# Sums moved into the slots' bank, the steps of a pass reordered, beginning and end rewritten: a graph-attention layer on one core

## The chip, the cores and the metric

The kernel runs on one core of a Trainium2 chip. The metric is the device time of one execution in microseconds (us). The core has a matrix engine (TensorE, "PE" in the profile, with its weight loads as "PEld"), three engines for element-wise work (VectorE "DVE", ScalarE "ACT", GpSimd "POOL") and SyncE ("SP"), which here only starts transfers. GpSimd starts the gathers: one instruction fetches 128 rows of 128 floats by 128 indices. TensorE writes its results into PSUM, which the kernel divides into banks of 128 x 512 floats; VectorE and ScalarE read them from there. Every engine works through its own instructions in order and waits for others by semaphores.

## The reference

12,500 nodes with 128 features, 200,000 edges sorted by target node, so about 16 edges per node. What is computed, cut to what matters:

```python
h = jnp.maximum(_layernorm(x, axis=-1), 0.0)
Qv = h @ W_Q.T;  Ku = h @ W_K.T
score = jnp.einsum('md,md->m', Qv[dst], Ku[src]) * (1.0 / np.sqrt(d))
score = score * jnp.exp(-edge_dt)
...                                   # per target node: keep the 16 best scores
w = jnp.where(keep, jnp.exp(score_m - seg_max[dst_s]), 0.0)
alpha = w / denom[dst_s]
msgs = h[src_s] @ W_msg.T
agg = segment_sum(alpha[:, None] * msgs, dst_s)
return x + jax.nn.relu(h @ W_self.T + agg)
```

## The kernel before

**Tiling.** The edges are cut into 1,563 chunks of 128, and 14 chunks (GC) make a group; there are G = 112 groups, the last one (L = 111) with 9 chunks. A group is also given the first chunk of the next one (NJ = 15), and it owns up to 128 target nodes. For every edge the row h[src] is gathered into the tile hs of its group (line 176, one instruction per chunk); eight such tiles exist.

**Preparation** (to line 421). `src` is loaded, cast (335), turned by TensorE and written as columns of indices (338). x is loaded in six blocks; VectorE takes row statistics (`row_stats`, line 200 and after), ScalarE the square root (212) and the normalised rows (`normed`, 220), and SyncE stores them as h_tab. The first four groups (RAW) don't wait for h_tab: their rows are gathered from x itself (`gather_at_once`) and normalised later in the tile (`raw_stats`, `raw_normed`). Then `dst` is turned into distances and places: `rel` (381), a running count (the scan, 386), and the table pd, with 16 places and 16 distances for every edge and group (397 and 400), which is made of transposes in TensorE's three "q" banks. The table is [edge, group, 2, 16], so that one write of many groups is strided.

**Passes** (lines 709 to 785). A software pipeline, written out by hand: the order of the calls in a pass is the order on every engine. Pass i works on several groups at once:

- group i + 2: node rows turned (`h_turned`, `h_turned_out`, line 517), then q = h A (`q_made`, `q_out`).
- group i + 1: the "eight steps of nodes and distances". Four `far_of` (TensorE to bank "a", line 534; ScalarE squares it out, 536), `edges_turned` (547, 550) and three `away` (557, 559). All go through the single bank "a", so each waits until ScalarE has read the step before. `to_edges` (541) and `places` (563) end them.
- group i: `q_to_edges` (574) carries q to the edges, `scores` (583) multiplies with the gathered rows and sums; `scores_in_slots` (591) spreads the scores over 40 slots.
- group i - 1: `slots_by_node` (599) sums the slots of each node into bank "e", columns 0 to 151; `slots_out` (604) and `node_by_slots` (607) turn them into columns 256 to 296 of the same bank.
- group i - 2: `best` (613 to 625) finds the 16 best, `sum_of_exps` (630), `kept_to_edges` (642), `one_over_sum`, `on_edges` (648 to 655) and `exps` bring the result back to the edges.
- group i - 3: `weights` (663, 664), then `sums` (674), the weighted sum of h[src] on TensorE, in bank "a" in two halves, and `sums_out` (679).
- groups i - 4 and i - 5: `sums_turned`, `products` (689, 690) in bank "s"; `output` (694) and `store` (700 on SyncE; 703 on GpSimd for the last four groups).

Between them `more(k)` lets gathers go: VectorE copies two columns of indices (191), and GpSimd starts two gathers. In pass i these are gathers of groups i + 4 and i + 5, for pass 3 the first of group 8, which takes over the tile of group 0. In the first four passes `raw_stats` and `raw_normed` for group i + 1 stand in the pass, and the entries of `later` (checks on the input, lines 440 to 451) are spread over passes 1 to 9. The loop runs to i = G + 5, so the last six passes only finish what is in the pipeline.

Lines 789 and after are a general path that is taken only if a check fails; it isn't taken here.

## Time and profile before

| | |
|---|---|
| time, median of 3 runs | 2059.91 us (2058.63 to 2059.99) |
| the profiled execution | 2061.69 us, of which its span is 2059.8 |
| granted TensorE clock, mean | 0.906 of full speed |
| busy: PE / PEld / DVE / ACT / POOL | 1641.5 / 1314.4 / 1274.5 / 1044.7 / 1513.8 us |
| first gather, last gather, last store started | 15.76, 2014.06, 2046.57 us |
| granted clock, 100 to 200 us | 0.73 |

A line of a group's table gives the line of the program, engine, operation, tiles and shapes, the count, the busy time and the mean duration in ns, and the idle time just before these instructions with what ended it. A line of a timeline gives the start and duration in us, then the same, and in brackets the idle time before and what ended it. L12 is line 12 of the kernel before.

### The profile page before, as it was taken

To read this page: it belongs to the slowest core of one execution; us is meant where nothing else is said; L and a number is where in the kernel's file an instruction comes from. 1 tells how busy PE (TensorE), PEld (TensorE's weight loads), DVE (VectorE), ACT (ScalarE), POOL (GpSimd) and SP (SyncE) were. 2 spreads that over 40 slices of the span, in tenths; PEclk is the share of its full clock that TensorE was granted. 3 is DMA by queue.
4 is the path that set the end of the run, shared out by engine and by line. 5 is a ranking of instruction groups with operands and counts; after the bars stand their busy time and mean duration, and the time that the engine had idled before them with its cause. 6 is when DMAs were issued, how large, how long until landed. Compare 5 with 4: busy or idle time off the path is not lost. (4 is left out here: it accounts for less than half of the span.)

```text
span 2059.8 us, 42100 instructions
## 1 busy us (share of the span) xinstructions
PE 1641.5 (80%) x13800; PEld 1314.4 (64%) x13801; DVE 1274.5 (62%) x6998; ACT 1044.7 (51%) x2198; POOL 1513.8 (73%) x1580
## 2 busy tenths in 40 slices
PE   0367899999887888888888888878888778888885
PEld 0246677777676766667666666766666666667664
DVE  7547767676666555565656666566556655666653
ACT  6756555565444554444544544454444544445440
POOL 6775777777777777777777777777777777777771
PEclk9958999999989898898989999899989998898987
DMA  9521222222222222222222222222222222222220
GB/s 237 158 57 46 74 69 64 69 65 68 65 63 63 64 66 64 64 65 65 65 65 65 65 64 63 64 65 65 65 65 65 65 65 65 65 65 63 64 55 16
DMA packets 101472, 143.46 MB, mean 70 GB/s; under 512 B 31063, under 2 KB 74327, under 8 KB 100480
## 3 DMA queue, kind: packets, MB, share of 16 engines
q0 software_dynamic: 50144, 102.74, 19.1%
q1 hardware_dynamic: 51102, 37.99, 6.7%
q8 instruction: 108, 1.77, 0.4%
q14 instruction: 118, 0.97, 0.2%
HBM read 126.79 MB, written 14.40 MB: 69 GB/s over the span
## 5 line engine op out<-in xcount | busy, mean ns | idle before, releaser
L176 POOL DMA_INDIRECT hs<-h_tab,ix x1507 | 1445.7, 959 | 475.4 <-issue 298.3
L583 DVE SCALAR_TENSOR_TENSOR prod<-hs,dec_all,q 128x128 f32<-128x128 f32 x1674 | 499.8, 344 | 193.0 <-DMA hs<-h_tab,ix 159.4
L574 PEld LDWEIGHTS q<-q,to_e 128*128 128x128 f32 x3348 | 477.4, 215 | 73.7 <-issue 59.6
L574 PE MATMUL q<-q,to_e 128*128 128x128 f32 x3348 | 520.4, 303 | 0.0
L536 ACT ACTIVATE far<-a,minus 128x512 bf16<-128x512 f32 (+1 forms) x447 | 295.2, 660 | 390.5 <-PE a L534 381.2
L674 PE MATMUL a<-hs,alz 128*128 128x128 f32 x3348 | 444.1, 288 | 11.5 <-ACT aw L559 0.4
L674 PEld LDWEIGHTS a<-hs,alz 128*128 128x128 f32 x3348 | 413.8, 201 | 22.6 <-ACT aw L559 19.2
L613 DVE TENSOR_SCALAR ell<-slots,e 128x40 f32<-128x40 f32 x112 | 29.7, 265 | 467.9 <-PE e L599 449.9
L599 PEld LDWEIGHTS e<-opo,sl 128*41 128x41 f32 x3348 | 177.3, 133 | 100.5 <-issue 89.4
L534 PE MATMUL a<-rel,ident 112*128 112x512 bf16 (+1 forms) x447 | 191.4, 428 | 44.1 <-ACT far L536 27.0
L559 ACT ACTIVATE aw<-a 128x400 bf16<-128x400 f32 x336 | 168.6, 502 | 106.8 <-PE a L557 106.8
L599 PE MATMUL e<-opo,sl 128*41 128x40 f32 x3348 | 217.8, 223 | 0.0
L541 ACT ACTIVATE to_e<-far 128x1920 f32<-128x1920 bf16 x112 | 200.5, 1790 | 0.0
L557 PE MATMUL a<-minus_at,pdT 32*128 32x400 bf16 x336 | 118.0, 351 | 95.2 <-ACT aw L559 78.8
L682 PE MATMUL s<-ident,agn 128*128 128x128 f32 x112 | 40.1, 358 | 172.1 <-DVE o L694 168.1
L679 ACT ACTIVATE agn<-a,rden 128x128 f32<-128x128 f32 x112 | 41.2, 368 | 198.3 <-PE a L674 198.3
L583 DVE DVE_READ_ACCUMULATOR prod<-hs,dec_all,q 128x1 f32 x1674 | 138.5, 83 | 0.0
L563 ACT ACTIVATE opo<-aw 128x1200 f32<-128x1200 bf16 x112 | 136.1, 1215 | 0.0
L682 PEld LDWEIGHTS s<-ident,agn 128*128 128x128 f32 x112 | 16.5, 147 | 185.4 <-DVE o L694 178.4
L191 DVE COPY ix<-idx_all 128x2 int32<-128x2 int32 x754 | 129.7, 186 | 0.0
L642 PEld LDWEIGHTS <-to_e 128*128 128x128 bf16 x1674 | 51.6, 99 | 100.3 <-DVE prod L583 86.9
L550 ACT CAST pdT<-a 32x128 bf16<-32x128 f32 x112 | 28.5, 254 | 157.5 <-PE a L547 157.5
(172 smaller groups left out, 1734.8 us busy)
## 6 DMA issues: line engine op xcount, KB each, us to landing
hs<-h_tab,ix POOLq DMA_INDIRECT x1507
h_r<-h_tab SPq DMA_DIRECT2D x112, 64.0 KB
x_t<-in_x_dram SPq DMA_DIRECT2D x108, 64.0 KB
out_dram<-o SPq DMA_DIRECT2D x108, 64.0 KB
xg<-in_x_dram SPq DMA_DIRECT2D x2, 1400.0 KB
h_tab<-xg SPq DMA_DIRECT2D x2, 1400.0 KB
xg<-in_x_dram SPq DMA_DIRECT2D x1, 1120.0 KB
h_tab<-xg SPq DMA_DIRECT2D x1, 1120.0 KB
```

The source lines that it names most:

```text
L176: nc.gpsimd.indirect_dma_start(out=T[g]["hs"][:, j, :], out_offset=None, in_=table[0:N, :], in_offset=bass.IndirectOffsetOnAxis(ap=index(j ...
L191: nc.vector.tensor_copy(ix[:, j0:j1], idx_all[:, GC * g + j0:GC * g + j1])
L534: nc.tensor.matmul(pr[:, 0:n1 - n0], lhsT=upper(ident[0:RR, g:g + 1]).to_broadcast([RR, P]), rhs=rel[:, n0:n1], start=True, stop=True)
L536: nc.scalar.activation(T[g]["far"][:, n0:n1], pr[:, 0:n1 - n0], AF.Square, bias=minus)
L541: nc.scalar.activation(T[g]["to_e"][:, 0:n], T[g]["far"][:, 0:n], AF.Relu, bias=1.0, scale=-1.0)
L557: nc.tensor.matmul(pr[:, 0:400], lhsT=T[g]["pdT"], rhs=minus_at.rearrange("k w j s -> k (w j s)")[:, n0:n1], start=True, stop=True)
L559: nc.scalar.activation(T[g]["aw"][:, n0:n1], pr[:, 0:400], AF.Square)
L563: nc.scalar.activation(T[g]["opo"].rearrange("e w j s -> e (w j s)"), T[g]["aw"], AF.Relu, bias=1.0, scale=-1.0)
L574: nc.tensor.matmul(pq[:, (j - j0) * P:(j - j0 + 1) * P], lhsT=T[g]["to_e"][:, j * P:(j + 1) * P], rhs=T[g]["q"], start=True, stop=True)
L583: nc.vector.scalar_tensor_tensor(prod, rows_of(g, j), dec_all[:, c:c + 1], T[g]["pq", b][:, (j % 4) * P:(j % 4 + 1) * P], op0=OP.mult, op1 ...
L599: nc.tensor.matmul(et[0:KM + 1, STEP * j:STEP * j + WN], lhsT=sl1[g % 2][:, j, :], rhs=T[g]["ow"][:, j, :], start=False, stop=(j == n - 1))
L674: nc.tensor.matmul(T[g]["pa"][:, 0:P], lhsT=alz[g % 2][:, WW * j + PRE:WW * j + PRE + P], rhs=rows_of(g, j), start=(j == 0), stop=(j == n ...
```

## The change

- **Beginning.** The GpSimd instructions that make `slots`, `nvec` and `jj` come ahead of those for `dst_r`. Memsets of w0, alz[0] and sl1 move behind the normalising of x, and most of the memset of pd is dropped. The cast of src is cut into 512 columns and the rest. The statistics of the first block of x follow the first gathers. `raw_stats` and `raw_normed` of groups 0 and 1 move out of the passes into the preparation; those of groups 2 and 3 become `raw_stats` and one tile (`raw_begun`) at the end of pass 0 and 13 tiles (`raw_finished`) at the end of passes 1 and 2.
- **Table turned.** pd is [edge, 32, group]: the writes of 397 and 400 are contiguous, and the columns that `edges_turned` loads are strided.
- **Passes.** `sums` goes to columns 384 to 511 of bank "e", so bank "a" serves only the eight steps, which spread over the pass; the three blocks of `slots_by_node` stand together; `node_by_slots` and `edges_turned` move to the middle of the pass, `sums_out` ahead of `products`; q has two buffers, not three.
- **End.** The loop stops after pass G - 2, and what remains is one written list.

```diff
--- before.py
+++ after.py
...
-    pd = const.tile([P, G, 2, 16], BF16, name="pd")
-    dlw = pd[:, :, 1, 0:NJ]
+    pd = const.tile([P, 32, G], BF16, name="pd")
+    dlw = pd[:, 16:16 + NJ, :].rearrange("e j g -> e g j")
...
-    def normed(rows, n, rs, sm):
-
-        nc.vector.reciprocal(rs, rs)
-        nc.vector.scalar_tensor_tensor(sm, sm, -0.5, rs, op0=OP.mult, op1=OP.mult)
-        for t in range(n):
+    def normed(rows, n0, n1, rs, sm):
+
+        if n0 == 0:
+            nc.vector.reciprocal(rs, rs)
+            nc.vector.scalar_tensor_tensor(sm, sm, -0.5, rs, op0=OP.mult, op1=OP.mult)
+        for t in range(n0, n1):
             nc.scalar.activation(rows[:, t, :], rows[:, t, :], AF.Relu, bias=sm[:, t:t + 1],
                                  scale=rs[:, t:t + 1])
+
+
+    def raw_stats(g):
+        T[g]["raw"] = row_stats(rows_pool, T[g]["hs"], own[g], f"r{g % 2}")
+
+    def raw_normed(g):
+        normed(T[g]["hs"], 0, own[g], *T[g]["raw"])
+
+
+    def raw_begun(g):
+        normed(T[g]["hs"], 0, 1, *T[g]["raw"])
+
+    def raw_finished(g):
+        normed(T[g]["hs"], 1, own[g], *T[g]["raw"])
...
         make_identity(nc, ident)
+        nc.gpsimd.iota(slots, pattern=[[1, KM]], base=0, channel_multiplier=0,
+                       allow_small_or_imprecise_dtypes=True)
+        nc.gpsimd.iota(nvec, pattern=[[0, 1]], base=0, channel_multiplier=1,
+                       allow_small_or_imprecise_dtypes=True)
+
+        jj, eq = (alz[0][0:32, NJ * KM * k:NJ * KM * (k + 1)].rearrange("p (j k) -> p j k", k=KM) for k in range(2))
+        nc.gpsimd.iota(jj, pattern=[[1, NJ], [0, KM]], base=0, channel_multiplier=0,
+                       allow_small_or_imprecise_dtypes=True)
         nc.gpsimd.iota(dst_r, pattern=[[1, RL + P]], base=1 << 21, channel_multiplier=0)
...
-        nc.gpsimd.iota(slots, pattern=[[1, KM]], base=0, channel_multiplier=0,
-                       allow_small_or_imprecise_dtypes=True)
-        nc.gpsimd.iota(nvec, pattern=[[0, 1]], base=0, channel_multiplier=1,
-                       allow_small_or_imprecise_dtypes=True)
...
-        nc.vector.memset(pd, 1.0)
+        for k in (15, 31):
+            nc.vector.memset(pd[:, k, :], 1.0)
+        nc.vector.memset(pd[:, GC:NJ, G - 1:G], 0.0)
         nc.vector.memset(dec_all[:, RR * CPR:CW], 0.0)
         nc.vector.tensor_scalar(minus, nvec, -1.0, None, op0=OP.mult)
-        for j in range(NJ):
-            nc.vector.memset(w0[:, j:j + 1], float(lead(j)))
...
-        nc.vector.memset(alz[0], 0.0)
-        for k in range(2):
-            nc.vector.memset(sl1[k][:, :, KM:], 1.0)
-
 
         src_f = src_r.bitcast(F32)[:, 0:RW]
-        nc.vector.tensor_copy(src_f, src_r[:, 0:RW])
-        stat = {0: row_stats(prep, xs[0][2], sizes[0], "x0")}
+        nc.vector.tensor_copy(src_f[:, 0:4 * P], src_r[:, 0:4 * P])
+        nc.vector.tensor_copy(src_f[:, 4 * P:], src_r[:, 4 * P:RW])
         by_chunk = lambda t: t[:, 0:RR * CPR].rearrange("e (p j) -> e j p", j=CPR)
         to_columns(src_f, 0, lambda at, p: nc.vector.tensor_copy(at(by_chunk(idx_all)), p))
-        for g in range(min(RAW, G)):
+        for g in range(RAW):
             gather_at_once(g, x)
+        stat = {0: row_stats(prep, xs[0][2], sizes[0], "x0")}
...
-            normed(xg, n, *stat[i])
+            normed(xg, 0, n, *stat[i])
...
+        for j in range(NJ):
+            nc.vector.memset(w0[:, j:j + 1], float(lead(j)))
+        nc.vector.memset(alz[0], 0.0)
+        for k in range(2):
+            nc.vector.memset(sl1[k][:, :, KM:], 1.0)
+        for g in range(2):
+            raw_stats(g)
...
+        raw_normed(0)
...
+        raw_normed(1)
...
-            nc.vector.tensor_tensor(dlw.rearrange("e g j -> e j g")[:, j0:j1, :],
+            nc.vector.tensor_tensor(pd[:, 16 + j0:16 + j1, :],
                                     pt[:, 0:(j1 - j0) * RR].rearrange("e (j g) -> e j g", g=RR),
                                     bc(w0[:, j0:j1], RR), op=OP.subtract)
-        to_columns(h1, HALO, lambda at, p: nc.scalar.copy(at(pd[:, :, 0, :].rearrange("e g j -> e j g")), p))
-        nc.scalar.copy(pd[:, 0:G - 1, 0, GC:NJ], pd[:, 1:G, 0, 0:1])
+        to_columns(h1, HALO, lambda at, p: nc.scalar.copy(at(pd), p))
+        nc.scalar.copy(pd[:, GC:NJ, 0:G - 1], pd[:, 0:1, 1:G])
...
-            T[g]["q"] = win.tile([P, D], F32, name="q", bufs=3)
+            T[g]["q"] = win.tile([P, D], F32, name="q", bufs=2)
...
-            nc.tensor.matmul(pr[0:32, 0:P], lhsT=pd[:, g, :, :].rearrange("e w j -> e (w j)"), rhs=upper(ident),
+            nc.tensor.matmul(pr[0:32, 0:P], lhsT=pd[:, :, g], rhs=upper(ident),
...
-            if part == 0:
-                T[g]["pa"] = bank("a", 1)
             half = n // 2
             for j in range(half) if part == 0 else range(half, n):
-                nc.tensor.matmul(T[g]["pa"][:, 0:P], lhsT=alz[g % 2][:, WW * j + PRE:WW * j + PRE + P],
+                nc.tensor.matmul(et[:, 384:384 + P], lhsT=alz[g % 2][:, WW * j + PRE:WW * j + PRE + P],
                                  rhs=rows_of(g, j), start=(j == 0), stop=(j == n - 1))
 
         def sums_out(g):
             T[g]["agn"] = win.tile([P, D], F32, name="agn")
-            nc.scalar.activation(T[g]["agn"], T[g]["pa"][:, 0:P], AF.Copy, scale=T[g]["rden"])
+            nc.scalar.activation(T[g]["agn"], et[:, 384:384 + P], AF.Copy, scale=T[g]["rden"])
...
-        for i in range(-3, G + 6):
+        for i in range(-3, G - 1):
...
-            if i + 1 < RAW:
-                at(i + 1, raw_stats)
-
...
             at(i, q_to_edges, 0)
-            at(i + 1, edges_turned)
             at(i - 5, output)
             at(i - 5, store)
             at(i - 3, weights)
@@ -741,48 +750,130 @@
...
             at(i, q_to_edges, 1)
             at(i + 1, far_of, 1)
-            at(i - 1, slots_by_node, 0)
+            for b in range(3):
+                at(i - 1, slots_by_node, b)
             at(i + 1, far_of, 2)
-            at(i - 1, slots_by_node, 1)
-            at(i + 1, far_of, 3)
-            at(i - 1, slots_by_node, 2)
-            at(i + 1, away, 0)
-            if i + 1 < RAW:
-                at(i + 1, raw_normed)
             more(1)
             at(i - 2, best)
             more(2)
             at(i - 2, sum_of_exps)
             at(i - 1, slots_out)
             at(i, q_to_edges, 2)
-            at(i + 1, away, 1)
+            at(i + 1, far_of, 3)
             at(i + 2, h_turned)
-            at(i + 1, away, 2)
             at(i, scores, 0)
             more(3)
             at(i + 1, to_edges)
             at(i + 2, h_turned_out)
             at(i - 2, kept_to_edges)
+            at(i - 1, node_by_slots)
+            at(i + 1, edges_turned)
             at(i - 3, sums, 0)
             at(i, scores, 1)
             more(4)
+            at(i + 1, away, 0)
             at(i, q_to_edges, 3)
             at(i - 2, one_over_sum)
+            at(i + 1, away, 1)
             at(i - 3, sums, 1)
             at(i, scores, 2)
             at(i - 2, on_edges)
             more(5)
+            at(i + 1, away, 2)
+            at(i - 3, sums_out)
+            at(i - 4, products)
+            at(i - 2, exps)
             at(i + 1, places)
-            at(i - 4, products)
-            at(i - 3, sums_out)
-            at(i - 2, exps)
             at(i, scores, 3)
             at(i, scores_in_slots)
+            if i == 0:
+                raw_stats(2)
+                raw_stats(3)
+                raw_begun(2)
+                raw_begun(3)
+            if i in (1, 2):
+                raw_finished(i + 1)
             more(6)
-            at(i - 1, node_by_slots)
             at(i + 2, q_made)
             if i > 0 and later:
                 later.pop(0)()
+
+
+        L = G - 1
+        blocks = -(-chunks[L] // 4)
+
+        def turned(g):
+            sums_turned(g)
+            sums_turned_out(g)
+
+        def all_sums(g):
+            sums(g, 0)
+            sums(g, 1)
+            sums_out(g)
+
+        def to_rows(g):
+            products(g)
+            output(g)
+            store(g)
+
+        def all_slots(g):
+            for b in range(3):
+                slots_by_node(g, b)
+
+        def to_nodes(g):
+            all_slots(g)
+            slots_out(g)
+            node_by_slots(g)
+
+        def kept_on_edges(g):
+            one_over_sum(g)
+            on_edges(g)
+            exps(g)
+
+        q_to_edges(L, 0)
+        output(L - 5)
+        store(L - 5)
+        weights(L - 3)
+        turned(L - 4)
+        all_slots(L - 1)
+        slots_out(L - 1)
+        best(L - 2)
+        sum_of_exps(L - 2)
+        q_to_edges(L, 1)
+        node_by_slots(L - 1)
+        to_rows(L - 4)
+        all_sums(L - 3)
+        kept_to_edges(L - 2)
+        best(L - 1)
+        sum_of_exps(L - 1)
+        scores(L, 0)
+        kept_on_edges(L - 2)
+        turned(L - 3)
+        kept_to_edges(L - 1)
+        scores(L, 1)
+        weights(L - 2)
+        all_sums(L - 2)
+        to_rows(L - 3)
+        for b in range(2, blocks):
+            q_to_edges(L, b)
+            scores(L, b)
+        scores_in_slots(L)
+        to_nodes(L)
+        kept_on_edges(L - 1)
+        turned(L - 2)
+        best(L)
+        sum_of_exps(L)
+        weights(L - 1)
+        kept_to_edges(L)
+        all_sums(L - 1)
+        to_rows(L - 2)
+        kept_on_edges(L)
+        turned(L - 1)
+        weights(L)
+        all_sums(L)
+        to_rows(L - 1)
+        turned(L)
+        to_rows(L)
     assert not later
     order.close()
 
```

More of the change, by code (lines that the diff above doesn't have):

```diff
@@ L112, in gnn_layer @@
     G = -(-CH // GC)
-    assert G > TAIL
+    assert G > TAIL + 2
     EG = GC * P
@@ L298, in gnn_layer @@
         load_rows(ew_r, ew)
-        nc.gpsimd.iota(slots, pattern=[[1, KM]], base=0, channel_multiplier=0,
-                       allow_small_or_imprecise_dtypes=True)
-        nc.gpsimd.iota(nvec, pattern=[[0, 1]], base=0, channel_multiplier=1,
-                       allow_small_or_imprecise_dtypes=True)
-        jj, eq = (alz[0][0:32, NJ * KM * k:NJ * KM * (k + 1)].rearrange("p (j k) -> p j k", k=KM) for k in range(2))
-        nc.gpsimd.iota(jj, pattern=[[1, NJ], [0, KM]], base=0, channel_multiplier=0,
-                       allow_small_or_imprecise_dtypes=True)
         nc.gpsimd.memset(alz[1], 0.0)
@@ L447, in gnn_layer @@
                                                op1=OP.mult, accum_out=badc[:, 2:3]),
-        lambda: nc.vector.tensor_reduce(badc[:, 0:1], pd[:, :, 0, 0:NJ], axis=AX.XY, op=OP.max),
+        lambda: nc.vector.tensor_reduce(badc[:, 0:1], pd[:, 0:NJ, :], axis=AX.XY, op=OP.max),
         lambda: nc.vector.tensor_scalar(badc[:, 0:1], badc[:, 0:1], float(KM), None, op0=OP.is_ge),
@@ L502, in load_nodes @@
                 nc.sync.dma_start(T[g]["x_t"], x_end[ds(start_of(g, 1, XT), P), :])
-        def raw_stats(g):
-            T[g]["raw"] = row_stats(rows_pool, T[g]["hs"], own[g], "r")
-        def raw_normed(g):
-            normed(T[g]["hs"], own[g], *T[g]["raw"])
         def h_turned(g):
```

## The prediction

> **What bounds the kernel now.** I read the page's table of groups first, then GpSimd's timeline, because one line of the table is 1,446 us long.
>
> ```profile
> L176 POOL DMA_INDIRECT hs<-h_tab,ix x1507 | 1445.7, 959 | 475.4 <-issue 298.3
> L583 DVE SCALAR_TENSOR_TENSOR prod<-hs,dec_all,q 128x128 f32<-128x128 f32 x1674 | 499.8, 344 | 193.0 <-DMA hs<-h_tab,ix 159.4
> ...
> L613 DVE TENSOR_SCALAR ell<-slots,e 128x40 f32<-128x40 f32 x112 | 29.7, 265 | 467.9 <-PE e L599 449.9
> ```
>
> A gather takes 0.96 us of GpSimd and 0.30 us to the next one, and the scores (L583) wait for gathered rows, 159.4 us in all. GpSimd's timeline shows where this queue is not full:
>
> ```profile
> 15.76 1.12 POOL L176 DMA_INDIRECT hs<-in_x_dram,idx_all  x1 [9.57 <-DVE idx_all L338]
> ...
> 164.59 0.95 POOL L176 DMA_INDIRECT hs<-h_tab,ix  x1 [0.30 <-issue]
> 179.84 0.95 POOL L176 DMA_INDIRECT hs<-h_tab,ix  x1 [14.30 <-ACT up L659]
> 182.90 1.44 POOL L176 DMA_INDIRECT hs<-h_tab,ix  x1 [2.12 <-issue]
> ...
> 2014.06 0.95 POOL L176 DMA_INDIRECT hs<-h_tab,ix  x1 [0.30 <-DVE km L623]
> 2030.19 1.01 POOL L703 DMA_INDIRECT out_dram<-o,idxo  x1 [15.19 <-DVE kept L663]
> ```
>
> From 182.9 to 2015.0 no idle stretch passes 0.5 us: 1,450 gathers x 1.25 = 1,812.6, plus 18.5 in gathers stretched by a VectorE instruction. So the span is three pieces: up to the gather at 179.84, a middle that only GpSimd sets, and what follows the last gather. The one hole is at 165.5: eight row tiles (hs) exist, the ninth group needs the first one's, and that is free when the sums of group 0 end. The name beside the 14.30 (L659) is a bystander; TensorE's timeline has the sums ending 177.32 + 1.95 = 179.27.
>
> ```profile
> 177.32 1.95 PE L674 MATMUL a<-hs,alz 128*128 128x128 f32 x16
> ...
> 2014.75 3.59 PE L674 MATMUL a<-hs,alz 128*128 128x128 f32 x30
> ...
> 2023.82 4.77 PE L674 MATMUL a<-hs,alz 128*128 128x128 f32 x30
> ...
> 2032.51 5.22 PE L674 MATMUL a<-hs,alz 128*128 128x128 f32 x30
> ```
>
> The last three are the sums of groups L-3, L-2 and L-1 (L = 111); L's follow, and the last store is issued at 2046.57.
>
> **The middle** (nothing). The pass in which eight steps share one bank less takes as long as 14 gathers, 17.5 us; at 182 to 480 us, while the passes catch up, it takes 14.2 to 14.7. The new order takes two blocks of slot sums out from between distance steps, so L613 starts perhaps 0.6 us earlier; the sums' bank, the one q buffer less and the strided table under L547 lie in the same slack. If that cover were gone, each 0.1 us over 17.5 would cost 10.7 us.
>
> **The front, step by step.** The rows of before that matter:
>
> ```profile
> 55.28 0.20 ACT L212 ACTIVATE rsx<-rsx 125x15 f32<-125x15 f32 x1
> ...
> 71.36 7.07 ACT L400 CAST pd<-q 128x448 bf16<-128x448 f32 x4 [9.00 <-PE q L272]
> ...
> 82.88 0.30 ACT L517 COPY hT<-s 128x128 f32<-128x128 f32 x1
> ...
> 153.66 5.48 ACT L220 ACTIVATE hs<-hs,smr,rsr 128x128 f32<-128x128 f32 x14
> ```
>
> First gather: VectorE drops the pd memset (3.04) and defers those of alz (2.06) and w0 (0.21); nvec comes before the 1.79 us iota, so the minus_at chain (3.4) ends near 6.0. By then 0.95 MB had been moved and src is the first 0.8 of it. Cast of 512 columns 0.3, four transposes 0.8, copy 0.8, start 0.5: the first gather near 9.5, 6.3 earlier. Worth nothing by itself: GpSimd reaches the hole at 159 instead of 165.5 and waits longer. SP's loads do pay: five gathers x 64 KB more among them at 235 GB/s are 1.4 us, and VectorE already waited 1.89 for the fifth block of x (33.8). I take the last sqrt from 55.3 to 57.0 (bounds 55 and 58).
>
> VectorE behind that sqrt: the memsets 2.3 and raw_stats of groups 0 and 1, 3.8 each by the row at 77.03 to 80.83, come before row, dst, rel and scan, which take the 10.3 us they took (55.9 to 66.2); two raw_normed add 0.45 each. L397 starts at 79.1, not 66.2, and takes four times 0.55 instead of 1.87 (no row writes this shape; L389 moves 224 columns in 0.38, L338 448 in 0.80; bounds 0.4 and 0.8). ScalarE: raw_normed(1) 5.4 from 78.9; the four pd casts 2.2 instead of 7.07 (L559 does 400 columns in 0.50), L401 0.25 instead of 1.02, table load 1.28, decays 2.84. The first hT copy ends at 91.1, against 83.2: **8 us later**, the saving of 9 on the turned table included.
>
> In return the passes lose two of four ScalarE blocks of 5.48 and the stats in between. Pass -1: 83 to 100.5 before, 11.8 us now, to 103. Pass 0 took 18.5 up to L563; less 5.48, plus 2 for the TensorE work that lay under that block, is 15: 118. But raw_stats(2) and (3), 7.6, now follow on VectorE, and ScalarE queues the sqrt and the first normed tile of each behind them: it stands from 118.5 to 126. TensorE, behind it, does eight products and one distance step ahead and then stops too. Pass 1: 12.4 before without the block, 15 now (three slot blocks in a row, 3.1 at the slow clock, hold up the third distance step); 141; raw_finished(2) 5.1: 146. Pass 2 likewise 16 with table load and exponentials, 162, plus 5.1: 167. Pass 3 to the end of the sums: 11 to 14. Cold TensorE gives 181, warm from 171 on 178; with every pass 1.5 shorter 175. I take **178.5: 0.8 us earlier than 179.27**, range 170 to 184. Let_go of the ninth group sits behind on_edges at the same point of the pass, near 179, so it is not later than the sums by more than a few tenths.
>
> **The tail.** Time from the end of the last gather (2015.0 before). VectorE finishes the slots of L-1 at -7.1 in both, since gather (L, 0) sets it. Before, from there: outputs at -7.2, 4.4, 14.1, 23.2, 27.0, 28.9 (L694), last store issued 31.6. The list, with the same rows: output(L-5) and weights(L-3) to -6.0; slots(L-1) on TensorE to -3.9; best(L-2) 2.2, to -1.7; all_sums(L-3) from -2.0, 3.6, to 1.7. **best(L-1)** reads the bank that those sums write: it starts at 1.8, not -1.4; to 4.0; scores(L,0) 5.2; kept_on_edges(L-2) 2.4, 7.6; scores(L,1) 8.7; weights(L-2) 9.6. all_sums(L-2) after idle stretches 4.8, to 14.4; products(L-3), output(L-3) 15.2. VectorE is in order, so scores(L,2), the slots of L, kept_on_edges(L-1) and best(L) all wait behind that output for 5 us (before, scores(L,2) was done at 2.0). Then 0.8 + 2.4 + 2.1 + 1.0 to weights(L-1) at 21.5; all_sums(L-1) 5.0, products 0.6, output(L-2) 27.4; only behind it kept_on_edges(L) 1.9, weights(L) 30.0 (before, on_edges(L) lay under sums(L-1)); sums 2.3, output(L-1) 33.0, turn and products, output(L) 34.8, against 29.2. **5.7 us later.** The stores keep their queues (L-4 and older on SP, the rest on GpSimd behind a finished gather queue), so the 2.4 from output to store stays.
>
> **Two rules weighed.** The row: L613 waits 449.9 us for L599, which writes other columns of its bank. The Trainium skill, *PSUM — Partial Sum Buffer*, section "PSUM bank collisions raise a hardware error", says to guard by bank and quadrant, not by address, and so speaks against moving sums into this bank. With it best(L-1) waits 3.2 us and the tail is 5.7 longer; by address alone it would be 2.5. The row decides. Second, the sums: 3.59 at a granted clock of 0.95 (2012 to 2018), 5.22 at 0.72 (2032 to 2038). *TensorE: Matmul & The Clock Gate*, Part 1, has the clock fall after an idle window of about 3.4 us. No gap in the list is that long, so by the rule the two sums would take 3.6 each: a tail of +3.1. But 4.77 followed an idle stretch of 2.14, so the rows' 4.8 and 5.0 stand.
>
> **Sum.** -0.8 + 0 + 5.7 = +4.9 on a span of 2059.8: 2064.7. That execution took 2061.69 in all, 1.8 above the median of 2059.91; on the median I forecast **2065**. The measurement can tell 0.2% (4.1 us) from no change.
>
> **Rivals.** *The tail as here, the front about even* (58%): 2065, own range 2060 to 2070; about a fifth of it falls within 0.2%. *The front wins* (17%): the sums of group 0 end near 168.5 because the passes 1 and 2 take 12 instead of 15 and 16 us, ScalarE being the only limit; GpSimd could use up to 20 (hole and earlier start): -10.8 + 5.7 gives 2055. For it: ScalarE is busy only 9.2 us of a pass. Against it: in those passes it waits for TensorE at 0.73 of its clock. It decides for faster once the sums end before 169.5. *The tail costs nothing* (15%): warm sums and best(L-1) not held, 2059; against it the two rows above. *The front loses too* (10%): pass 3 cold and a later x phase put the sums at 184.5, +5.2 + 5.7, 2071. That the turned table brings nothing costs 9 more and belongs here.
>
> **Numbers.** Slower by over 0.2%: 0.45 of the first and 0.10 of the last, 0.55. Faster: 0.14 of the second and 0.04 of the third, 0.18. Within 0.2%: 0.27. For 8 in 10 I take 2052 to 2071: the second case's better half below and half the last above are left out.
>
> **What would show it.** First gather near 9.5; L397 and L400 near 0.55 each; first L517 near 91; the hole still there, the gather behind it near 179; from there to the last gather 1,831 +- 4; last store about 37 after the last gather, with VectorE idle some 5 us before output(L-3) and output(L-2). Wrong if the hole closes before 170, if passes in the middle exceed 17.5, or if the list ends within 32 of the last gather.

## The result, and the profile after

The changed kernel takes **2052.3 us** (median of eight runs, 2049.6 to 2053.8) against 2059.6 for the kernel before (eight runs, 2058.6 to 2060.3): a ratio of **0.9964, interval 0.9953 to 0.9974**. It is faster by 0.36%, where the forecast was 2065. The runs below were made on several chips; on one of them the kernel before itself takes 2865 us at a granted clock of 0.76, and the four runs made there are said to be of the slow chip.

The page's table of groups has the same leader as before, with fewer microseconds in it:

```profile
L176 POOL DMA_INDIRECT hs<-h_tab,ix x1507 | 1439.9, 955 | 464.9 <-issue 303.5
...
L598 DVE SCALAR_TENSOR_TENSOR prod<-hs,dec_all,q 128x128 f32<-128x128 f32 x1674 | 508.0, 343 | 298.2 <-DMA hs<-h_tab,ix 260.0
...
L628 DVE TENSOR_SCALAR ell<-slots,e 128x40 f32<-128x40 f32 x112 | 28.4, 254 | 369.8 <-PE e L614 319.0
```

L176 is the gather (L176 before too), L598 the scores (L583 before), L628 the first step of best (L613 before). The scores now wait 260 us for gathered rows instead of 159, and the idle time before L628 is 370 us instead of 468: VectorE is early more often, and has to wait for GpSimd. GpSimd's timeline gives the three pieces of the forecast (start, duration, in brackets the idle time before and what ended it):

```profile
10.23 1.12 POOL L176 DMA_INDIRECT hs<-in_x_dram,idx_all  x1 [3.87 <-DVE idx_all L349]
...
171.11 2.60 POOL L176 DMA_INDIRECT hs<-h_tab,ix  x1 [5.75 <-DVE ix L191]
174.17 0.95 POOL L176 DMA_INDIRECT hs<-h_tab,ix  x1 [0.46 <-issue]
...
1995.29 0.94 POOL L176 DMA_INDIRECT hs<-h_tab,ix  x1 [0.30 <-issue]
...
2034.76 0.98 POOL L716 DMA_INDIRECT out_dram<-o,idxo  x1 [2.01 <-issue]
```

The gather behind the hole starts at 171.11 instead of 179.84 (**-8.7**; forecast -0.8). From it to the last gather it is 1824.2 us instead of 1834.2 (**-10.0**; forecast 0). From the end of the last gather to the last store it is 38.5 instead of 31.6 (**+7.0**; forecast +5.7). With -0.2 behind the store this is the difference of the two spans, 2047.8 and 2059.8. GpSimd comes to the hole at 165.4 (171.11 less the 5.75 of idle time), no earlier than before, where the forecast had 159. That execution was the fastest of its eight, so the medians differ by 7.3 and not by 12.

For the middle I sorted the 1,450 intervals between the starts of gathers, in every trace below, in two: those under 1.28 us, whose mean is the pace of GpSimd alone, and the **long** ones, whose surplus over that pace is the excess. Before: 45 long, 20.4 us of excess. After: 21 and 11.9. (Each count holds the one interval of 3.06 behind the hole, which all kernels have.) Most long intervals (41 before, 17 after) are gathers that started while VectorE ran one product of two SBUF inputs over 600 columns: the slots by scores (L591 before, L606 after) or the weights (L664, L679). Two pairs from the timeline of before, each a product of VectorE and the gather that GpSimd started under it. The product of the first pair, L653, is as long as the other, but one of its inputs lies in PSUM:

```profile
300.08 0.77 DVE L653 TENSOR_TENSOR mine<-x,opo 128x600 f32<-128x600 f32 x1
...
300.19 0.95 POOL L176 DMA_INDIRECT hs<-h_tab,ix  x1 [0.30 <-issue]
...
302.57 0.79 DVE L591 TENSOR_TENSOR sl<-opo,s 128x600 f32<-128x600 f32 x1
...
302.69 1.49 POOL L176 DMA_INDIRECT hs<-h_tab,ix  x1 [0.30 <-DVE prod L583]
```

Both gathers begin 0.11 to 0.12 us behind their product. The first lasts 0.95 us as ever, the second 1.49.

### The profile page after: what moved, and what is told of

It reads as the page before. It is cut to its first block, busy times and chain, and to the rows that moved or that the text cites. A ratio compares the mean times of both kernels' runs of the same rounds, so it can differ in the third digit from the quotient of the medians.

```text
span 2047.8 us, 42217 instructions
## 1 busy us (share of the span) xinstructions
PE 1581.4 (77%) x13800; PEld 1304.9 (64%) x13801; DVE 1281.2 (63%) x7001; ACT 1026.3 (50%) x2198; POOL 1508.7 (74%) x1580
## 5 line engine op out<-in xcount | busy, mean ns | idle before, releaser
L176 POOL DMA_INDIRECT hs<-h_tab,ix x1507 | 1439.9, 955 | 464.9 <-issue 303.5
L598 DVE SCALAR_TENSOR_TENSOR prod<-hs,dec_all,q 128x128 f32<-128x128 f32 x1674 | 508.0, 343 | 298.2 <-DMA hs<-h_tab,ix 260.0
L589 PEld LDWEIGHTS q<-q,to_e 128*128 128x128 f32 x3348 | 484.7, 214 | 34.1 <-DVE prod L598 13.5
L687 PE MATMUL e<-hs,alz 128*128 128x128 f32 x3348 | 436.7, 284 | 4.6 <-DVE alz L679 4.6
L687 PEld LDWEIGHTS e<-hs,alz 128*128 128x128 f32 x3348 | 394.9, 193 | 32.0 <-issue 19.2
L628 DVE TENSOR_SCALAR ell<-slots,e 128x40 f32<-128x40 f32 x112 | 28.4, 254 | 369.8 <-PE e L614 319.0
L549 PE MATMUL a<-rel,ident 112*128 112x512 bf16 (+1 forms) x447 | 196.1, 439 | 14.8 <-ACT far L551 14.8
L614 PE MATMUL e<-opo,sl 128*41 128x40 f32 x3348 | 189.8, 230 | 0.9 <-DVE rden L650 0.9
L598 DVE DVE_READ_ACCUMULATOR prod<-hs,dec_all,q 128x1 f32 x1674 | 136.8, 82 | 0.0
L657 PE MATMUL x<-km,to_e 128*128 128x43 bf16 x1674 | 61.4, 184 | 70.9 <-DVE km L640 66.0
L606 DVE TENSOR_TENSOR sl<-opo,s 128x600 f32<-128x600 f32 x112 | 87.5, 782 | 3.9
```

Source lines behind the costliest of these rows:

```text
L176: nc.gpsimd.indirect_dma_start(out=T[g]["hs"][:, j, :], out_offset=None, in_=table[0:N, :], in_offset=bass.IndirectOffsetOnAxis(ap=index(j ...
L549: nc.tensor.matmul(pr[:, 0:n1 - n0], lhsT=upper(ident[0:RR, g:g + 1]).to_broadcast([RR, P]), rhs=rel[:, n0:n1], start=True, stop=True)
L589: nc.tensor.matmul(pq[:, (j - j0) * P:(j - j0 + 1) * P], lhsT=T[g]["to_e"][:, j * P:(j + 1) * P], rhs=T[g]["q"], start=True, stop=True)
L598: nc.vector.scalar_tensor_tensor(prod, rows_of(g, j), dec_all[:, c:c + 1], T[g]["pq", b][:, (j % 4) * P:(j % 4 + 1) * P], op0=OP.mult, op1 ...
L614: nc.tensor.matmul(et[0:KM + 1, STEP * j:STEP * j + WN], lhsT=sl1[g % 2][:, j, :], rhs=T[g]["ow"][:, j, :], start=False, stop=(j == n - 1))
L687: nc.tensor.matmul(et[:, 384:384 + P], lhsT=alz[g % 2][:, WW * j + PRE:WW * j + PRE + P], rhs=rows_of(g, j), start=(j == 0), stop=(j == n ...
```

## The experiments

All in one table first, for the readings that return: the start of the gather behind the hole; the long intervals and their excess; the mean of the other intervals; from the end of the last gather to the last store; the span of the profiled execution; the median of all runs. "slots' bank" is e, "distances' bank" is a.

```
kernel               hole   long/excess  others   tail   span     median
before              179.84   45 / 20.4   1.2509   31.6   2059.8   2059.6
after               171.11   21 / 11.9   1.2498   38.5   2047.8   2052.3
e_after_again       172.10   24 / 12.5   1.2506   40.2   2052.1   2054.0
e_end_loop          173.83   17 / 11.2   1.2483   30.9   2040.1   2048.1
e_order_only        177.75   20 / 10.2   1.2485   31.3   2043.4   2046.6
e_begin_only        175.67   43 / 21.0   1.2485   32.7   2053.7   2057.2
e_bank_only         179.93   46 / 14.9   1.2510   32.1   2054.8   2057.8
e_table_only        174.73   48 / 20.2   1.2507   33.6   2056.1   2055.8
e_raw_only          182.90   50 / 21.9   1.2484   30.8   2060.1   2062.1
e_split_before_2    179.75   57 / 10.0   1.2485   31.7   2045.9   2048.5
e_put_off_2         170.76  100 / 19.8   1.2513   41.3   2060.5   2059.0
e_new_list_2        170.25   22 / 13.0   1.2484   26.2   2034.0   2036.6
e_order_list        174.86   21 /  9.6   1.2483   25.5   2034.4   2039.1
e_new_list_split    169.59   32 /  7.9   1.2486   25.1   2027.0   2031.7
```

The kernel before, run beside the others on each chip, took 2059.7 us (rows e_end_loop to e_bank_only), 2057.9 (e_split_before_2 to e_order_list) and 2058.8 (the other four), so that medians of different chips can be compared within 2 us. The other columns are of one trace each. The three traces of the same beginning and passes (after, e_after_again, e_end_loop) have the hole's end at 171.1 to 173.8, and the two of the order alone (e_order_only, e_order_list) at 177.8 and 174.9, so a difference of 2 or 3 us at the hole is not told from chance.

**The end alone undone.**

```
-        for i in range(-3, G - 1):
+        for i in range(-3, G + 6):
...
-        L = G - 1
...
-        to_rows(L)
```

> The changed kernel with its written end undone: the loop of passes runs out to the last output as it did before, the rest of the change stays. Three-piece theory (the beginning gave 8.7, the pass order 10 in the middle, the written end lost 7): last store issued about 31.5 after the last gather instead of 38.5, 2045 us in all. Rival (the end is longer because the sums now lie in the slots' bank, or because TensorE is slower after the last gather, and the list is innocent): last store still 37 to 39 after the last gather, 2052.

2048.1 us, ratio to before 0.9942 (0.9928 to 0.9955); tail 30.9. The list is the loser, not the bank by itself: with the sums in the slots' bank and the loop's end the tail is even 0.7 shorter than before. The time came out 3 above the expected.

**The order of the pass alone**, and with it, on the other side, **the bank alone**: the kernel before with

```
-            if part == 0:
-                T[g]["pa"] = bank("a", 1)
...
-                nc.tensor.matmul(T[g]["pa"][:, 0:P], lhsT=alz[g % 2][:, WW * j + PRE:WW * j + PRE + P],
+                nc.tensor.matmul(et[:, 384:384 + P], lhsT=alz[g % 2][:, WW * j + PRE:WW * j + PRE + P],
```

and in the first the calls of the pass in the changed kernel's order too.

> The kernel before with nothing but the new order of the pass and the sums in the slots' bank; beginning, table and end loop as before. Theory (the order takes stretched gathers out of the middle): hole ends at 180 as before, some 20 gathers of over 1 us with 12 us of excess instead of 41 with 18, second gather to last gather near 1821, 2050 us, up to 2 more if the end loop suffers from the shared bank. Rival (the number of stretched gathers follows from the phase in which the middle begins, thus from the beginning): 41 or so stretched, 1831, 2059.

> The kernel before with nothing but the sums moved from the distances' bank to the slots' bank, order of the pass unchanged. Theory (the order matters, not the bank): middle 1829 to 1833, 2059 to 2062. Rival (distance steps held up behind the sums of the old bank make the passes late, so the bank alone brings the middle's gain): middle near 1821, 2050.

The order with the bank: 2046.6 us, ratio 0.9937 (0.9923 to 0.9951), more than the whole change brings. Long intervals fall from 45 to 20, the excess by 10.2. The bank alone: 2057.8 us, ratio 0.9991 (0.9982 to 0.9999), with as many long intervals, though shorter ones: in its one trace the excess is 5.5 less, about half of what order and bank bring together. By the medians it is worth 1.9 us of the 13.1. So the greater part of the time comes with the order; how the middle's own gain is divided between the two, one trace of each does not settle. Not expected: the order brings the hole forward too.

```profile
177.75 1.20 POOL L176 DMA_INDIRECT hs<-h_tab,ix  x1 [11.24 <-PE a L557]
```

It is 2.1 us earlier here, and 5.0 in e_order_list, which is the same up to that point. The first hT copy ends at 83.7 as before (83.2), the second at 96.4 instead of 99.9: the first pass is shorter by 4.

**What stretches a gather.** Two runs, each a direct attempt on the product. One cuts both products in three pieces of 200 columns in the kernel before:

```
+            for a in range(0, n, 5):
+                b = min(a + 5, n)
+                nc.vector.tensor_tensor(sl1[g % 2][:, a:b, 0:KM], T[g]["po"][:, a:b, :],
+                                        bc(T[g]["s"][:, a:b], KM), op=OP.mult)
```

> As e_split_before, for a chip on which the kernel before takes about 2060 us and GpSimd sets the middle. Theory (a gather that starts while a VectorE product of two SBUF inputs runs waits for its end): excess of the long gathers from 20 to under 5 us, middle 1834 to 1817 to 1819, 2044 us. Rival (three products back to back keep the gather out as one does): excess 16 to 22, 2059. Second rival (the passes of before hang by so little that four instructions more, 0.3 us a pass, make them late): middle over 1834, 2062 or more.

The other moves the slots' product later in the changed kernel:

```
+            for k in range(2):
+                put_off = win.tile([P, D], F32, name="prod")
+                nc.vector.tensor_copy(put_off, T[g]["pq", 0][:, P * k:P * (k + 1)])
             nc.vector.tensor_tensor(sl1[g % 2][:, 0:n, 0:KM], T[g]["po"][:, 0:n, :],
```

> As e_put_off, for a chip on which the kernel before takes about 2060 us. Theory (what counts is where in the 1.25 us of a gather the slots' product starts): moved 0.4 us later, most of the products that began 0.5 to 1.0 us ahead of the next gather begin 0.1 to 0.6 ahead of it; 60 or more long gathers, 10 to 25 us more excess than the changed kernel's 12, 2062 to 2077. Rival (the phase is of no account): about 20 long gathers, 2052.

The split: 2048.5 us, ratio 0.9962 (0.9949 to 0.9976), by halving the excess, although the three pieces take 0.92 us where one product took 0.78. There are not fewer long intervals, but each is shorter. The theory had under 5 us of excess and 2044: the pieces still hold gathers, for a shorter time. The delay: 100 long intervals, over 90 of them under the slots' product, 7.5 us more excess than the changed kernel and 7 to 8 us more time (ratio to before 1.0005, interval 0.9996 to 1.0014, against 0.9972 and 0.9964 of the change). The direction is the theory's, the size below its 10 to 25: the copies moved the product by only some 0.2 us, so that most gathers met its last 0.3 us. A typical pair (the product of VectorE, then the gather of GpSimd):

```profile
1028.37 0.77 DVE L609 TENSOR_TENSOR sl<-opo,s 128x600 f32<-128x600 f32 x1
...
1028.86 1.10 POOL L176 DMA_INDIRECT hs<-h_tab,ix  x1 [0.31 <-issue]
```

Sorted by the time from the start of such a product (0.78 us) to the start of the next gather, the traces give a law: number of pairs, and mean duration of the gather in us.

```
start of gather behind
start of product, us     -0.3..0.0   0.1       0.2       0.3       0.4      0.5       0.6       0.7       0.8       0.9
before                   26 / 0.95   14/1.50   14/1.40    4/1.30    3/1.20   2/1.07    7/0.99   52/0.95   57/0.95   35/0.94
after                    19 / 0.98    4/1.75    6/1.40    3/1.28    1/1.22      -      6/0.98   53/0.94   86/0.94   36/0.94
e_put_off_2              20 / 0.98    1/1.56    5/1.39    2/1.28    5/1.16  55/1.07   27/1.02   91/0.95    8/0.95      -
```

A gather that starts from 0.04 to 0.62 us behind the start of the product ends 1.6 us behind that start, that is 0.8 behind the product's end (the 1.75 of after has one gather that was held twice). One that starts before the product or up to 0.04 us behind it is not touched, and then the product is the longer one, up to 0.85 us. It is not the length of the VectorE instruction that counts: under L653 and its like in the other two, 600 columns and 0.77 us with one input from PSUM, 271 gathers of these three traces started 0.05 to 0.6 us behind the start, and all took 0.94 to 0.96 us. In the kernel before, 35 pairs fall between 0.1 and 0.4; in the changed one 14. Why they are fewer is argued, not shown: with more of its waits for gathered rows (260 us instead of 159) VectorE comes to the product in the gathers' own rhythm, 0.7 to 0.9 ahead of the next one.

The Trainium skill has this port (*SBUF — State Buffer*, section "Who interferes with whom"): an instruction of VectorE with two SBUF inputs contends with a GpSimd instruction that reads SBUF; the shared ports are an exclusive lock, and the order of issue decides who waits. These numbers agree with that. The section also infers that a `tensor_tensor` leaves GpSimd's making of descriptors alone; here the gather as a whole is held (1.49 us for 0.95), and whether in its reading of indices or in its making of descriptors, these runs do not separate.

**The end: what in the list loses.** On the slow chip three ends can be compared from the start of the sums of L-3 to the last store, a stretch in which GpSimd waits in any case: e_put_off with the list as changed, e_tail_bank with the last sums in the distances' bank, e_new_list with another list besides.

```
+            if part == 0:
+                T[g]["pa"] = et[:, 384:384 + P] if g < L - 3 else bank("a", 1)[:, 0:P]
```

```
         scores(L, 1)
+        for b in range(2, blocks):
+            q_to_edges(L, b)
+            scores(L, b)
+        scores_in_slots(L)
+        turned(L - 3)
+        kept_to_edges(L - 1)
+        to_nodes(L)
         weights(L - 2)
+        kept_on_edges(L - 1)
         all_sums(L - 2)
+        best(L)
+        sum_of_exps(L)
+        weights(L - 1)
+        kept_to_edges(L)
         to_rows(L - 3)
+        kept_on_edges(L)
         turned(L - 2)
...
```

(The places further down from which these steps were taken are left out.)

> The changed kernel with the sums of the last four groups (L-3 to L) in the distances' bank, which nothing else uses there; the written end itself unchanged. Step of the forecast (best(L-1) waits for the sums of L-3 because both lie in one bank): best(L-1) starts at about -1 instead of +2 after the last gather, tail 38.5 - 3.2 = 35.3, 2049. Rival (behind it VectorE only waits longer for output(L-3)): best(L-1) earlier by 3, tail 37.5 to 38.5, 2052.

> The changed kernel with the last sums in the distances' bank and another written end: group L's last products, scores and slots, kept_on_edges(L-1) and best(L) are taken ahead of output(L-3) and of the sums of L-2 where they can be, kept_on_edges(L) ahead of output(L-2). Theory (what lengthened the end is that VectorE, and TensorE ahead of it, queue L's steps behind output(L-3) and output(L-2)): last store issued 24 to 28 after the last gather, 2039 to 2042. Rival (the four sums at 5 to 6 us each on a slow TensorE set the end): 31 to 35, 2045 to 2049.

43.4, 37.5 and 27.7 us; 40.4 in the changed kernel's own trace (1994.33 to 2034.76). best(L-1), which waited 3.1 us for the sums of L-3 in e_put_off, starts in e_tail_bank 1.0 us after they have begun. The end is 2.9 shorter than the changed kernel's, whose later sums take the same time on TensorE (6.12, 4.82 and 3.26 us against 6.14, 4.82 and 3.25); of the 5.9 to e_put_off, 2.7 are slower sums there (6.27, 6.39 and 4.21). So the bank is worth about what the forecast said, 3.2, though this compares one trace each, of two chips or of a kernel with the two copies added. The larger part, 9.8 from e_tail_bank to e_new_list, is the order of VectorE and TensorE behind output(L-3). The same list on a chip like the first:

> As e_new_list, for a chip on which the kernel before takes about 2060 us. On the slow chip the time from the start of the sums of L-3 to the last store was 27.7 us with it, against 37.5 with the written end and the sums in the distances' bank and 43.4 with both as changed. Theory: the changed kernel's 40.4 there becomes 28, tail 26, 2052 - 12 = 2040. Rival (the end of a GpSimd-bound run starts later in the pass, so that L's steps have nothing to lie under): tail 31 to 35, 2045 to 2049.

**2036.6 us, ratio 0.9900 (0.9885 to 0.9915)**, tail 26.2 as expected, the time 3 below. Its last sums, on TensorE:

```profile
1993.20 3.51 PE L691 MATMUL a<-hs,alz 128*128 128x128 f32 x30
...
2002.63 5.24 PE L691 MATMUL a<-hs,alz 128*128 128x128 f32 x30
2009.24 3.51 PE L691 MATMUL a<-hs,alz 128*128 128x128 f32 x30
2014.29 2.27 PE L691 MATMUL a<-hs,alz 128*128 128x128 f32 x18 [0.25 <-DVE alz L679]
```

Of the four only those of L-2 are still slow; in the changed kernel those of L-1 took 4.82 and those of L 3.26.

**The beginning, whole and in parts.** e_begin_only is the kernel before with the beginning and the table of the changed one; e_order_list is e_new_list without them; e_table_only and e_raw_only are the kernel before with one part each:

```
-    pd = const.tile([P, G, 2, 16], BF16, name="pd")
-    dlw = pd[:, :, 1, 0:NJ]
+    pd = const.tile([P, 32, G], BF16, name="pd")
+    dlw = pd[:, 16:16 + NJ, :].rearrange("e j g -> e g j")
```

```
+        for g in range(2):
+            raw_stats(g)
...
         let_go(RAW, 2)
+        raw_normed(0)
...
+            if i == 0:
+                raw_stats(2)
+                raw_stats(3)
+                raw_begun(2)
+                raw_begun(3)
```

> The kernel before with nothing but the new beginning: earlier iotas, fewer memsets, raw rows of groups 0 and 1 normalised before the passes and of 2 and 3 at the ends of passes, turned table; one q buffer less. Old pass order, sums in their old bank, end loop. Theory: the gather behind the hole starts near 172 instead of 179.8, the middle stays 1831, tail 31.6: 2051.5. Rival (the new order of the pass is what made the passes -1 to 3 short): hole ends at 177 to 180, 2057 to 2060. Second rival (the middle's 10 us come from the beginning's phase): 2042.

> The kernel before with the new order of the pass and the end list of e_new_list, but with the old beginning and the old table. Theory (the three pieces add up, and the beginning gains 4 to 6): 4 to 6 us slower than e_new_list_2, 2045. Rival (the beginning gains nothing behind the new order, as 2046.6 for the order alone against 2048.1 with the beginning suggests): the same within 1.5 us, or faster, 2039 to 2041.

> The kernel before with nothing but the turned table (pd as 32 planes of G columns); all its memsets, the raw rows and the order stay. The forecast took its 9 us (L397 and L400, 16.6 us of casts in before's chain ahead of the first pass) as won in full ahead of the first hT copy. Theory (the casts lie on the chain to the passes): first hT copy at 74 to 76 instead of 82.9, gather behind the hole at 171 to 173, 2051. Rival (behind the casts the passes wait for the raw rows of groups 0 to 3, and what the table wins is lost there): hole ends at 176 to 179.8, 2055 to 2059.

> The kernel before with nothing but the raw rows moved: statistics of groups 0 and 1 ahead of the edges' rows on VectorE, 2 and 3 at the end of pass 0, normalising of 2 and 3 at the ends of passes 1 and 2; one q buffer less; table, memsets and iotas as before. The forecast had 8 + 9 us more ahead of the first hT copy, and the passes -1 to 2 shorter by 5.7, 3.5 less 8, 0 and 0: hole ends at about 188, 2067. Theory from the traces (the passes win 3.3 us more than that): first hT copy at 97 to 100, hole ends at 180 to 185, 2060 to 2065. Rival (the move alone is what made the front shorter): hole ends before 177, 2055.

At the hole, in one trace each, the table alone gains 5.1 us, the raw rows alone lose 3.1 (their first hT copy ends at 92.8, ahead of the 97 to 100 expected), the whole beginning gains 4.2 behind the old order and 4.6 behind the new. The table's two lines on ScalarE in e_table_only:

```profile
70.17 0.78 ACT L400 CAST pd<-q 128x448 bf16<-128x448 f32 x2 [0.21 <-PE q L272]
75.86 0.27 ACT L517 COPY hT<-s 128x128 f32<-128x128 f32 x1 [0.56 <-issue]
```

The first hT copy ends at 76.1 instead of 83.2: 7.1 us won, 2.0 of them lost again in the passes 0 to 2, between that run's theory and its rival. The theory of e_begin_only, that the beginning alone makes the front 8 us shorter, falls: 4.2 came, and 6 to 10 only where the new order is there too.

In the whole time less arrives: ratios 0.9987 (0.9977 to 0.9996) for the beginning, 0.9984 (0.9975 to 0.9993) for the table, 1.0006 (0.9995 to 1.0016) for the raw rows, which is not told from no change. Behind the new order it is not told from nothing. With the new list the kernel with it is 2.5 us faster by the medians (e_new_list_2 against e_order_list), where the theory had 4 to 6; with the loop's end it is 1.5 slower (e_end_loop, 2048.1, against e_order_only, 2046.6), and both pairs of intervals overlap. The traces of the first pair show 4.6 at the hole, and 3.4 more excess of long gathers behind it, of which 1.8 lies between the hole and 360 us. In e_begin_only and e_table_only 1.1 and 2.0 are given back at the end. Why, the traces do not settle.

**The change once more, and the best version.** e_new_list_split is e_new_list with the products cut as above.

> The changed kernel unchanged, beside the three others on one chip. If its profiled 12 us less than before are the kernel's and not one execution's: hole ends at 171 to 174, long gathers 17 to 25 with 10 to 13 us of excess, tail 38 to 39; 2050 to 2053.

> e_new_list with the slots' and the weights' products each in three pieces of 200 columns, as in e_split_before. Theory (the gain of the split is what stretched gathers are left): excess of the long gathers from 13 to about 7 us (the 3 at the first gather behind the hole stays), 4 to 6 us faster than e_new_list, 2031 to 2033. Rival (in the new order the pieces, 0.14 us longer in sum, move the phase and find new gathers): 2036 or more.

The change again: ratio 0.9972 (0.9962 to 0.9981); hole and long intervals as expected, the tail 40.2 and the time 2054.0 a little above. The best version: **2031.7 us, ratio 0.9867 (0.9852 to 0.9882)**, 27 us faster than before and 22 faster than the change. The excess is 7.9, of which the interval behind the hole is 1.8, and 3.4 lie under the long VectorE instructions of `later` (far_from_start and its followers, over 1,680 columns).

**The slow chip.** e_split_before and e_put_off ran there too.

> The kernel before with the two products of two SBUF inputs on VectorE, slots by scores (L591) and weights (L664), each cut from 600 columns into three of 200, back to back; the work is the same. Theory (a gather that starts while such an instruction runs waits for its end, and nothing else stretches it): gathers of over 1 us fall from 40 to under 10, the excess from 20 us to under 5, the middle from 1834 to 1817 to 1819, 2044 us, although VectorE runs four instructions more in each pass. Rival (back to back VectorE keeps the gather out all the same): excess 16 to 22, 2059. Second rival (the stretched gathers are a symptom of late passes and not of these instructions): the same 40 gathers, longer by other causes.

> The changed kernel with two copies of 128 columns from PSUM put ahead of the slots' product (L606) in VectorE's order, so that it starts some 0.4 us later against the gathers; the copies go to no use. Theory (what counts is where in the 1.25 us of a gather that product starts): most of the 88 products that begin 0.5 to 1.0 us ahead of the next gather now begin 0.1 to 0.6 ahead of it, 60 or more stretched gathers, 10 to 25 us more excess, 2062 to 2077. Rival (VectorE has 0.4 us to spare in a pass and the phase is of no account): about 20 stretched gathers, 2052.

With before at 2865: e_split_before 2942, e_put_off 3163, e_tail_bank 3154, e_new_list 3145. Neither of the two theories is tested, since gathers do not set the time. The page of e_tail_bank:

```profile
L176 POOL DMA_INDIRECT hs<-h_tab,ix x1507 | 1456.0, 966 | 1509.7 <-PE e L691 593.2
...
L574 ACT ACTIVATE aw<-a 128x400 bf16<-128x400 f32 x336 | 169.4, 504 | 1084.9 <-remote 622.9
```

The page's row of slices has the granted clock at 0.6 to 0.7 for nearly all of the span (mean 0.74). GpSimd stands idle for 1509.7 us, most of it until sums have freed a row tile; ScalarE and VectorE wait some 3 to 8 us at a time for something that the page calls "remote" and that no engine of the trace shows. What it is stays open. What can be said is that there GpSimd is not the bound, and that the three kernels with the change's beginning and order lose 10% to before, 2.6 us in each of the 112 passes. The changed kernel itself did not run there. So the gains above hold for chips on which the kernel before takes about 2060 us.

## Why the prediction was wrong, step by step

**The middle, "nothing": the step that failed.** The pass is hidden under the gathers, as the forecast had it, but the gathers themselves were not a constant. The forecast named the 18.5 us "in gathers stretched by a VectorE instruction" and then treated them as given. The change moves that instruction against the gathers: 8.5 us less excess in the first trace, 10.2 with the order and the bank alone. The other 1.5 of the 10 are the pace of GpSimd, which differs between executions of one kernel. With the front and the tail as measured and the middle at nothing, the span would have been 1.9 us shorter, which is no change; the sign came from the middle.

**The front: its chain right, its size wrong by 8.** The hole does end with the sums of group 0, as forecast. The forecast put the first hT copy at 91.1 and the end of the sums of group 0 at 178.5; they end at 86.5 and at 170.6.

```profile
53.60 0.20 ACT L212 ACTIVATE rsx<-rsx 125x15 f32<-125x15 f32 x1
...
80.46 1.61 ACT L422 CAST pd<-q 128x448 bf16<-128x448 f32 x4
...
86.21 0.30 ACT L532 COPY hT<-s 128x128 f32<-128x128 f32 x1
```

The mis-sized terms: the last sqrt of x is at 53.6, 1.7 earlier than before, and the forecast had it 1.7 later. This term differs between traces of the same beginning: 54.9 in e_after_again, 57.1 in e_end_loop, close to the 57.0 of the forecast. The casts take 1.6 instead of 2.2. Together with the rest this is 4.6 at the first pass. The other 3.3 are the passes: passes 1 and 2, for instance, take 13.7 and 14.2 instead of 15 and 16. In e_end_loop, where the sqrt came as forecast and the first hT copy ends at 90.1, the sums of group 0 end at 173.3, still 5.2 early, and 4.2 of these are the passes. The forecast priced the new order for its three slots' blocks in a row and gave it no gain; e_order_only and e_order_list show one of 2 and 5. The hole was still there, as foretold, but 5.75 long, where 159 to 179 would be 20: the gathers' earlier start, 5.5 us, was lost again ahead of the hole, 2.3 in waits and 3.2 in longer gathers. The rival "the front wins" had the shorter passes, and 12 us for them; with the tail as measured it alone would have given about 2058, no change.

**The tail: right, and 1.3 short, in part by a gap that the forecast did not see.** VectorE's timeline of after has the three idle stretches in the places forecast, best(L-1), output(L-3) and output(L-2):

```profile
1998.28 0.25 DVE L628 TENSOR_SCALAR ell<-slots,e 128x40 f32<-128x40 f32 x1 [3.46 <-ACT agn L692]
...
2012.38 0.29 DVE L707 SCALAR_TENSOR_TENSOR o<-s,x_t 128x128 f32<-128x128 f32 x1 [6.72 <-ACT agn L692]
...
2024.05 0.29 DVE L707 SCALAR_TENSOR_TENSOR o<-s,x_t 128x128 f32<-128x128 f32 x1 [5.43 <-ACT agn L692]
```

best(L-1) starts at +2.05 (forecast 1.8), the outputs end at +16.4 and +28.1 (15.2 and 27.4). On TensorE the mis-sized term:

```profile
2002.92 0.73 PE L657 MATMUL x<-km,to_e 128*128 128x43 bf16 x15 [4.29 <-DVE mine L668]
2005.71 6.12 PE L687 MATMUL e<-hs,alz 128*128 128x128 f32 x30 [2.05 <-DVE alz L679]
...
2026.99 3.26 PE L687 MATMUL e<-hs,alz 128*128 128x128 f32 x18 [2.20 <-DVE alz L679]
```

6.1 and 3.3 us, where the forecast had 4.8 and 2.3. Of the two rules weighed, the first was weighed the right way: the bank's guard holds (about 3 us in e_tail_bank). In the second the forecast's ground was wrong, "no gap in the list is that long": TensorE stands idle for 4.29 us shortly before the sums of L-2, which is above the 3.4 of *TensorE: Matmul & The Clock Gate*, Part 1, and these sums then run at a granted clock of 0.57. The slow sums of L-1 and L (0.73 and 0.66) have no idle stretch over 2.5 us shortly before them, so a gap of 3.4 is not needed. Nor does a gap of 2 us always bring slow sums: in the kernel before, those of L-2 took 4.77 us at a clock of 0.74 behind an idle stretch of 2.14, and in e_begin_only 3.59 at 1.00 behind one just as long:

```profile
2018.83 0.55 PE L657 MATMUL x<-km,to_e 128*128 128x43 bf16 x15 [2.14 <-DVE km L640]
2019.22 3.59 PE L689 MATMUL a<-hs,alz 128*128 128x128 f32 x30
```

That the forecast's 4.8 and 5.0 came near was thus in part luck.

**The chances.** Faster had 0.18, from cases in which the front or the tail went better. The case that came, a front that gains most of what the second case had, a tail somewhat longer and a middle that gains, was not among them.

## What to carry to other kernels

When one engine's queue sets the time, look at the spread of its own instructions before calling its stretch a constant: here 45 of 1,450 gathers carried 20 us, and cutting the instruction that stretched them was worth 9 us. A written order at the end is judged by what is queued behind its waits on each engine: moving the last group's steps ahead of two waiting outputs, with a bank of their own for the last sums, was worth 12 to 14 us of the tail, and leaving them behind cost 7 to 9. Take a change apart before it is kept or thrown away: the order with its bank gained 13, the beginning 2.5 by itself and nothing sure behind the order, the end lost 4 to 7, and together they looked like 5 to 7.

## What was not expected of the hardware

- A gather that starts 0.04 to 0.62 us behind the start of a 0.78 us VectorE product of two SBUF inputs ends 0.8 us behind the product's end; one that starts earlier is not held, and a product of the same length with one input from PSUM holds none (271 pairs in three traces).
- The pace of the undisturbed gathers is not the same in each execution: 1.2483 to 1.2513 us, mostly near one of the two ends, which is up to 4 us over 1,450 of them. It does not follow the kernel (after: 1.2498 and 1.2506; e_end_loop, the same passes: 1.2483). Its cause was not looked for.
- Sums of 30 products take 3.5 us where the granted clock stays at 1.00 and 6.1 where its mean is 0.57. The idle stretch just before them does not tell which: behind 2.14 us both 3.59 and 4.77 came.
